# Attention in a two-layer transformer kernel: the context product three heads behind the scores

## The chip, the cores and the metric

The kernel runs on one core of one Trainium2 chip. Its metric is the time on the device in microseconds, from the start of the program to its end. Before the change three runs gave 2274.1, 2275.8 and 2278.2 us; the median is 2275.79 us. The engines are named as the profile names them: PE is TensorE (matrix products; PEld is its loading of weights), DVE is VectorE, ACT is ScalarE, POOL is GpSimd, and SP is SyncE, which only issues transfers (DMAs).

## The reference, cut to what matters

The program is a block of two layers on x of shape 4 x 512 x 512 (4 batch entries, 512 tokens, 512 channels). Layer 0 is a state-space mixer and a mixture of experts; layer 1 is the attention that the change touches and a gated feed-forward net. Ahead of each of these four parts stands a gate computed from a second input by forward and backward scans. The attention, with 16 heads in 4 groups that share keys and values, is:

```python
q = einsum('bsh,he->bse', x, w_q).reshape(b, sq, GROUPS, HPG, KVC)     # 4 groups x 4 heads x 128
kv = einsum('bsh,he->bse', x, w_kv); k, v = split(kv, 2, axis=-1)      # 4 groups x 128 each
scores = einsum('bqgpd,bkgd->bgqpk', q, k) * KVC ** -0.5
scores = where(causal, scores, -inf)
probs = softmax(scores, axis=-1)
ctx = einsum('bgqpk,bkgd->bqgpd', probs, v).reshape(b, sq, HEADS * KVC)
return einsum('bse,eh->bsh', ctx, w_dense)                             # added to x
```

All of it is in 32-bit floats. The output is x after the four parts, each added to it.

## The kernel before, in words

Activations lie with channels on the 128 partitions: x[b] is a tile of 128 x 4 x 512, and h is the gated input of the attention in the same form.

The attention walks a list of 64 heads, `heads_` (line 1737): for each group g of 4, for each batch entry b of 4, for each head i of 4 within the group. One group of one batch entry, four heads, is called a unit here. For each unit `start_group` (line 1585) makes the keys (`pk`, 8 matrix instructions) and values (`pv`, 32). For each head

- `queries` (line 1612) makes the scaled queries, tile `pq`, 8 instructions;
- `scores` (line 1626) works in four steps qi over rows of 128 queries. The causal part only is computed: step qi has (qi + 1) x 128 columns. Each step is a product into a PSUM tile `psc`; VectorE adds the mask and takes the negative row maximum; ScalarE takes the exponential and its row sum; VectorE scales the row and transposes it in blocks of 32 x 32 into an SBUF tile `turned` (two of these). Between the maximum and the exponential stands `nudge()`, which issues one small step of the gates for later parts (their loads kt, ek and ekv on SP, scans on VectorE, exponentials on ScalarE) and sends finished gates off;
- a transpose of 128 x 128 is not complete with blocks of 32. The rest is done on the way through DRAM: four DMAs on POOL's queue write `turned` to a DRAM tile, one of the `turned_d` (line 1661), and one DMA on SP's queue reads it back as `pT` (line 1678). `pT` has two buffers;
- `context` (line 1682) multiplies `pT` with the values, tile `pctx`, 8 instructions, and ScalarE copies the result to `cx`;
- after the fourth head of a unit `dense` (line 1713) multiplies the four `cx` with the dense weights, tile `pd`, 32 instructions, and VectorE adds the result to x[b].

What is delayed against what is written out by hand in the main loop (lines 1756 to 1776). In the pass of head n the queries of head n + 1 come first, then the scores of head n, then `settle()` for the oldest head of the list `held`, once this has more than two: so the context is written two heads behind the scores. `collect()` reads back all that has been written; it stands in `scores` ahead of step 2, so head n - 1 is read back in the middle of the scores of head n. The last two heads of all take another way: their probabilities stay in SBUF and TensorE transposes them.

In group 0 the pass of head 1 of a batch entry also adds the results of the experts to x[b + 1] (`combine`), and the pass of head 2 loads and applies the gate that makes the next h (`gated`, a 1 MB load on SP). The dense weights have one buffer; the next group's are loaded in the pass of head 2 of its first batch entry, after the last `dense` of the group before.

The written order is not the order in which an engine runs. The framework in which the kernel is written orders the instructions of each engine and each queue itself, adds the waits between them, and starts from the order of the code; the trace shows what came out. Where the code says `with after(...)`, the instructions inside are kept behind the last ones of the engines named.

Of the kernel before, what the change touches and what calls it, by code (L numbers as in the profile page):

```python
# [10 lines left out]
F32 = mybir.dt.float32  # L11
# [72 lines left out]
def block_kernel(ctx: ExitStack, tc: tile.TileContext, a: dict, out: bass.AP):  # L84
    nc = tc.nc

    @contextmanager
    def after(*engines):

        with ExitStack() as es:  # L90
            for e in engines:
                last = next(
                    (i for i in reversed(nc.cur_bb.bb.instructions) if i.engine == e.engine), None
                )
                if last is not None:
                    es.enter_context(tc.issue_after(last))
            yield
# [38 lines left out]
    dr = ctx.enter_context(tc.tile_pool(name="spill", bufs=1, space=bass.MemoryType.DRAM))  # L136
# [6 lines left out]
    def ps_mm(name):  # L143
        return ps.tile([P, 512], F32, tag="mm", name=name, bufs=4)

    def ps_tp(name):
        return ps.tile([P, 512], F32, tag="tp", name=name, bufs=2)

    def ps_acc(name):
        return ps.tile([P, 512], F32, tag="acc", name=name, bufs=2)  # L150
# [239 lines left out]
    def nudge():  # L390
        old = list(unsent)
        next(making, None)
        if old:
            send()
# [16 lines left out]
    def gated(l, b, xb, pool, part=slice(0, T), **kw):  # L411
        have((l, b))
        n = part.stop - part.start
        g = pool.tile([P, NC, n], F32, **kw)
        nc.sync.dma_start(out=g, in_=gts[l][b][:, :, part])
        apply_gate(g, xb[:, :, part])
        return g
# [479 lines left out]
    with ExitStack() as ph:  # L897
# [23 lines left out]
        def lend_halves():  # L921

            left = []
            def take():
                if not left:
                    t = sm.tile([P, 8, P], F32, tag="lm", name="lm", bufs=3)
                    left.extend(t[:, i : i + 4, :].rearrange("p a b -> p (a b)") for i in (0, 4))
                return left.pop(0)
            return take
# [15 lines left out]
        turned, lend_turned = [], lend_halves()  # L945
# [556 lines left out]
    def combine(b):  # L1502

        for t in range(NT):
            add_results(b, t, load_results(b, t, nc.sync))
# [46 lines left out]
    with att as ph:  # L1552
# [10 lines left out]
        def load_dense(g):  # L1563
            w = HPG * KVC
            wd = wdp.tile([P, HPG, C], F32, tag="wd", name="wd")
            nc.sync.dma_start(
                out=wd, in_=a["w_dense"][g * w : (g + 1) * w, :].rearrange("(k p) m -> p k m", p=P)
            )
            return wd

        SQ, SLOTS = 32, 13
        QUAD = P // SQ
        turned = [mp.tile([P, QUAD, SLOTS, SQ], F32, name=f"turned{i}") for i in range(2)]
        for blocks in turned:
            for lo, hi in ((1, 3), (5, 6)):
                nc.gpsimd.memset(blocks[:, :, lo:hi, :], 0.0)
        turned_d = [dr.tile([QUAD, SQ, QUAD, SLOTS * SQ], F32, name=f"turned{i}") for i in range(3)]

        hs = [gp.tile([P, NC, T], F32, tag="h", name="h2")] + [None] * (B - 1)
        nc.sync.dma_start(out=hs[0], in_=early_h)  # L1580
# [45 lines left out]
        def scores(u, i, qT):  # L1626

            turn = u.last_row and i >= HPG - 2
            prs = []
            if not turn:  # L1630
                blocks = turned[next(numbers) % 2]
            for qi in range(NT):
                n = (qi + 1) * P
                if qi == 2:
                    collect()
                psc = ps_mm("psc")
                nc.tensor.matmul(  # L1637
                    psc[:, :n], lhsT=qT[:, qi * P : n], rhs=u.kT[:, :n], start=True, stop=True
                )
                nc.vector.tensor_tensor(psc[:, qi * P : n], psc[:, qi * P : n], mask, ALU.add)  # L1640
                nmax = sm.tile([P, 1], F32, tag="nmax", name="nmax", bufs=4)
                nc.vector.tensor_reduce(nmax, psc[:, :n], AX.X, ALU.max, negate=True)  # L1642
                with after(nc.vector, nc.scalar):
                    nudge()
                pr = sm.tile([P, n], F32, tag=f"pr{qi}", name="pr")
                rsum = sm.tile([P, 1], F32, tag="rsum", name="rsum", bufs=4)
                act(pr, psc[:, :n], AF.Exp, bias=nmax, accum_out=rsum)
                nc.vector.reciprocal(rsum, rsum)
                nc.vector.tensor_scalar(pr, pr, rsum, None, ALU.mult)  # L1649
                if turn:  # L1650
                    prs.append(pr)
                    continue
                nc.vector.transpose(  # L1653
                    blocks[:, :, 3 * qi : 4 * qi + 1, :].rearrange("p c k j -> p k c j"), pr
                )
            if turn:
                return prs
            d = turned_d.pop(0)
            turned_d.append(d)
            for r in range(QUAD):  # L1660
                nc.gpsimd.dma_start(  # L1661
                    out=d[:, :, r].rearrange("c i s -> i c s"),
                    in_=blocks[r * SQ : (r + 1) * SQ].rearrange("i c k j -> i c (k j)"),
                )
            away.append(d)
            return d

        away, back = [], {}

        def new_pT():  # L1670
            return sm.tile([P, QUAD, SLOTS, SQ], F32, tag="pT", name="pT")

        def collect():

            while away:
                d = away.pop(0)
                back[id(d)] = pT = new_pT()
                nc.sync.dma_start(
                    out=pT.rearrange("p r k j -> p (r k j)"), in_=d.rearrange("c i r s -> (c i) (r s)")
                )  # L1680

        def context(u, prs):

            if isinstance(prs, list):
                pT = new_pT()
                for qi, pr in enumerate(prs):
                    n = (qi + 1) * P
                    ptp = ps_tp("ptp")
                    for kj in range(qi + 1):
                        nc.tensor.transpose(  # L1690
                            ptp[:, kj * P : (kj + 1) * P], pr[:, kj * P : (kj + 1) * P], ident
                        )
                    nc.any.tensor_copy(
                        pT[:, :, 3 * qi : 4 * qi + 1, :].rearrange("p r k j -> p k r j"),
                        ptp[:, :n].rearrange("p (k r j) -> p k r j", r=QUAD, j=SQ),
                    )
            else:
                collect()
                pT = back.pop(id(prs))
            pctx = ps_acc("pctx")  # L1700
            for kj in range(NT):
                nc.tensor.matmul(  # L1702
                    pctx[:, kj * P :].rearrange("p (q r j) -> p q r j", r=QUAD, j=SQ),
                    lhsT=u.v[:, kj, :],
                    rhs=pT[:, :, 4 * kj : 10 + kj : 3, :].rearrange("p r q j -> p q r j"),
                    start=(kj == 0),
                    stop=(kj == NT - 1),
                )
            cx = sm.tile([P, T], F32, tag="cx", name="cx", bufs=5)
            nc.scalar.copy(cx, pctx)  # L1710
            u.ctxT.append(cx)
# [27 lines left out]
        def begin(n):  # L1739
            g, b, i = heads_[n]  # L1740
            if i == 0:
                if b == 0 and g + 1 < GROUPS:
                    weights[g + 1] = load_group(g + 1)
                groups[g, b] = start_group(g, b, weights[g])
            return groups[g, b], queries(groups[g, b], i)
# [9 lines left out]
        ready, held = begin(0), []  # L1755
        for n, (g, b, i) in enumerate(heads_):
            u, qT = ready
            if g == 0 and i == 1 and b + 1 < B:
                combine(b + 1)
            if g == 2 and i == 0 and b < 3:  # L1760
                to, name = ((ffg_d, "gateT"), (ffu_d, "upT"), (ffd_d, "downT"))[b]
                nc.sync.dma_start(out=to, in_=a[name])
            if g and b == 0 and i == 2:
                dense_w[g] = load_dense(g)
            if n + 1 < len(heads_):
                ready = begin(n + 1)
            if g == 0 and i == 2 and b + 1 < B:
                act.use(act.EXP)
                hs[b + 1] = gated(2, b + 1, x[b + 1], gp, tag="h", name=f"h2_{b + 1}")
                act.use(act.LOG_EXP)  # L1770
            prs = scores(u, i, qT)
            held.append((u, prs))
            if len(held) > 2:
                settle()
        while held:
            settle()
# [213 lines left out]
```

## Time and profile before

| What | us |
|---|---|
| Three runs, median (lowest to highest) | 2275.79 (2274.1 to 2278.2) |
| The profiled execution, its own time | 2278.28 |
| Its span in the profile | 2276.6 |
| Attention stage, from the first pk to the last pd | 1136 to 2031 |
| PE busy in that stage | 860.84 |
| VectorE busy in that stage | 587.84 |
| ScalarE busy in that stage | 340.72 |
| Feed-forward part after it | 2031 to 2277 |
| Median from the issue of a write `turned` to its landing | 3.9 |

The mean granted clock of TensorE over the whole execution is 0.979 of full speed, and 0.99 over the attention stage. The page gives each engine's busy time as a share of the span; a list of waits gives, for each engine and line, what ended its idle time, the total, how many times, and the longest. A timeline gives start, length, engine, line, operation, the tile written and those read, the number of instructions merged into the row, and in brackets the idle time of the engine just before with what ended it. For SP and POOL the rows are the issuing of transfers, not the transfers.

### The profile page before, as it was taken

The page shows a single profiled execution, that of the slowest core. Times are in us where ns is not written, and L with a number is a line of the kernel's source. Part 1 is how long each engine was busy: PE and PEld are TensorE (multiplying, and loading weights), DVE is VectorE, ACT ScalarE, POOL GpSimd, SP SyncE. Part 2 cuts the span into 40 slices and gives each one's busy share as a digit, 9 for nine tenths or more (in the row PEclk, how much of TensorE's full clock was granted, in tenths as well). Part 3 has the DMA queues.
Part 4 walks back from the last instruction along what each step waited for, and adds up shares of the span by engine and source line. Part 5 has one row for each costly group of instructions (what it writes and reads, how often), then busy time and mean ns, then how long its engine had stood idle before and what let it go on. Part 6 is the DMA issues. An engine that isn't in the chain of part 4 may idle for free. (4 is left out here: it accounts for less than half of the span.)

```text
span 2276.6 us, 23890 instructions
## 1 busy us (share of the span) xinstructions
PE 2134.7 (94%) x7528; PEld 1226.5 (54%) x7528; DVE 1524.0 (67%) x3041; ACT 972.2 (43%) x1900; POOL 417.2 (18%) x558
## 2 busy tenths in 40 slices
PE   2879999999999999999989999999999999999998
PEld 1545565555655444444444455555555555568887
DVE  8698989989642665566567766566667765456332
ACT  4476666766732233233254434333333333243222
POOL 4023232421332111111211111111111111100000
PEclk9889989999999999999999999999999999999999
DMA  7542341432523548978675566446545464441100
GB/s 261 169 141 75 102 158 66 153 121 65 186 76 136 190 164 298 341 273 277 209 249 179 172 191 186 139 138 190 167 143 158 139 196 142 131 184 38 37 19 20
DMA packets 112452, 357.38 MB, mean 157 GB/s; under 512 B 14592, under 2 KB 23168, under 8 KB 102912
## 3 DMA queue, kind: packets, MB, share of 16 engines
q1 hardware_dynamic: 87584, 277.26, 36.0%
q0 software_dynamic: 22432, 74.34, 11.1%
q10 hardware_dynamic: 2304, 4.20, 0.5%
q8 instruction: 62, 1.02, 0.2%
q14 instruction: 70, 0.57, 0.1%
HBM read 337.91 MB, written 108.00 MB: 196 GB/s over the span
## 5 line engine op out<-in xcount | busy, mean ns | idle before, releaser
L1661 POOL DMA_DIRECT2D turned<-turned x248 | 135.4, 552 | 713.7 <-DVE turned L1653 435.6
L1615 PE MATMUL pq<-h,wq 128*128 128x512 f32 x512 | 235.4, 597 | 2.0 <-DVE h L404 1.7
L1717 PE MATMUL pd<-cx,wd 128*128 128x512 f32 x512 | 223.3, 594 | 0.0
L128 ACT ACTIVATE pr<-psc,nmax 128x128 f32<-128x128 f32 (+3 forms) x256 | 134.7, 526 | 168.9 <-DVE nmax L1642 168.3
L1048 PE MATMUL pc<-h,wxb 128*128 128x512 f32 x320 | 148.6, 620 | 44.3 <-DVE h L1307 39.2
L1637 PE MATMUL psc<-kT,qT 128*128 128x128 f32 (+3 forms) x512 | 158.2, 442 | 14.5 <-ACT pr L128 14.5
L1702 PE MATMUL pctx<-pT,v 128*128 128x512 f32 (+3 forms) x512 | 153.3, 443 | 13.7 <-DMA pT<-turned 13.3
L1640 DVE TENSOR_TENSOR psc<-psc,mask 128x128 f32<-128x128 f32 x256 | 70.4, 283 | 140.5 <-PE psc L1637 140.3
L1717 PEld LDWEIGHTS pd<-cx,wd 128*128 128x128 f32 x512 | 96.5, 191 | 115.3 <-issue 110.1
L1702 PEld LDWEIGHTS pctx<-pT,v 128*128 128x128 f32 x512 | 98.1, 193 | 98.0 <-issue 67.0
L1615 PEld LDWEIGHTS pq<-h,wq 128*128 128x128 f32 x512 | 94.4, 192 | 100.9 <-issue 93.7
L811 PE MATMUL pg<-w,hT 128*128 128x512 f32 x296 | 136.0, 601 | 6.9 <-ACT hT L784 6.8
L844 PE MATMUL po<-w,yT 128*128 128x512 f32 x296 | 135.9, 600 | 6.2 <-ACT yT L837 6.2
L822 PE MATMUL pn<-w,hT 128*128 128x512 f32 x296 | 133.3, 592 | 0.0
L1725 DVE TENSOR_TENSOR xr<-xr,pd 128x512 f32<-128x512 f32 x64 | 43.8, 685 | 126.6 <-PE pd L1717 126.6
L1637 PEld LDWEIGHTS psc<-kT,qT 128*128 128x128 f32 x512 | 86.2, 192 | 73.6 <-ACT pr L128 31.1
L1048 PEld LDWEIGHTS pc<-h,wxb 128*128 128x128 f32 x320 | 61.8, 198 | 116.4 <-issue 74.5
L1642 DVE TENSOR_REDUCE nmax<-psc 128x1 f32<-128x128 f32 (+3 forms) x256 | 122.7, 480 | 1.9
L1653 DVE STREAM_TRANSPOSE turned<-pr 128x128 f32<-128x128 f32 x248 | 120.8, 498 | 1.4
L1710 ACT COPY cx<-pctx 128x512 f32<-128x512 f32 x64 | 37.2, 581 | 187.5 <-PE pctx L1702 187.5
L1119 PE MATMUL pz<-wzt,h 128*128 128x512 f32 x256 | 115.2, 598 | 0.3 <-ACT st L1220 0.3
L1267 PE MATMUL po<-wot,yT 128*128 128x512 f32 x256 | 115.2, 604 | 0.0
(343 smaller groups left out, 4198.0 us busy)
## 6 DMA issues: line engine op xcount, KB each, us to landing
w<-in_w1x SPq DMA_DIRECT2D x76, 1024.0 KB
turned<-turned POOLq DMA_DIRECT2D x248, 208.0 KB, 3.9
pT<-turned SPq DMA_DIRECT2D x62, 832.0 KB
w<-in_w2x SPq DMA_DIRECT2D x38, 1024.0 KB
wb<-in_b1x SPq DMA_DIRECT2D x38, 512.0 KB
lm<-cs SPq DMA_DIRECT2D x32, 512.0 KB
kt<-in_fT SPq DMA_DIRECT2D x62, 256.0 KB
ek<-ek SPq DMA_DIRECT2D x62, 256.0 KB
```

Source lines behind the costliest of these rows:

```text
L128: nc.scalar.activation(*args, **kw)
L811: nc.tensor.matmul(pg, lhsT=hT[:, k, :], rhs=self.w1[s][0][:, k, :], start=(k == 0), stop=(k == NC - 1))
L822: nc.tensor.matmul(pn, lhsT=hT[:, k, :], rhs=self.w1[s][1][:, k, :], start=(k == 0), stop=(k == NC - 1))
L844: nc.tensor.matmul(po, lhsT=yT[:, j, :], rhs=self.w2[s][:, j, :], start=(j == 0), stop=(j == NI - 1))
L1048: nc.tensor.matmul(pc, lhsT=wxb[:, k, m * P : (m + 1) * P], rhs=h[:, k, :], start=(k == 0), stop=(k == NC - 1),)
L1615: nc.tensor.matmul(pq, lhsT=u.wq[:, k, i * KVC : (i + 1) * KVC], rhs=u.h[:, k, :], start=(k == 0), stop=(k == NC - 1),)
L1637: nc.tensor.matmul(psc[:, :n], lhsT=qT[:, qi * P : n], rhs=u.kT[:, :n], start=True, stop=True)
L1642: nc.vector.tensor_reduce(nmax, psc[:, :n], AX.X, ALU.max, negate=True)
L1653: nc.vector.transpose(blocks[:, :, 3 * qi : 4 * qi + 1, :].rearrange("p c k j -> p k c j"), pr)
L1661: nc.gpsimd.dma_start(out=d[:, :, r].rearrange("c i s -> i c s"), in_=blocks[r * SQ : (r + 1) * SQ].rearrange("i c k j -> i c (k j)"),)
L1702: nc.tensor.matmul(pctx[:, kj * P :].rearrange("p (q r j) -> p q r j", r=QUAD, j=SQ), lhsT=u.v[:, kj, :], rhs=pT[:, :, 4 * kj : 10 + kj : ...
L1717: nc.tensor.matmul(po, lhsT=dense_w[u.g][:, i, m * P : (m + 1) * P], rhs=u.ctxT[i], start=(i == 0), stop=(i == HPG - 1),)
```

## The change

`held` now keeps three heads, so the context of head n - 3 is written after the scores of head n. `collect` takes a number of written heads that it leaves for later; in `scores` it stands ahead of step 0 and leaves one, so head n - 2 is read back at the start of the scores of head n. `context` calls `collect` only when its own probabilities have not been read back yet. A fourth DRAM tile holds the written probabilities. The dense weights of a group are loaded in the pass of head 3 instead of head 2, after the last `dense` of the group before, which comes one head later too.

```diff
-        turned_d = [dr.tile([QUAD, SQ, QUAD, SLOTS * SQ], F32, name=f"turned{i}") for i in range(3)]
+        turned_d = [dr.tile([QUAD, SQ, QUAD, SLOTS * SQ], F32, name=f"turned{i}") for i in range(4)]
...
             for qi in range(NT):
                 n = (qi + 1) * P
-                if qi == 2:
-                    collect()
+                if qi == 0:
+                    collect(1)
...
-        def collect():
+        def collect(rest=0):
 
-            while away:
+            while len(away) > rest:
                 d = away.pop(0)
                 back[id(d)] = pT = new_pT()
...
             else:
-                collect()
+                if id(prs) not in back:
+                    collect()
                 pT = back.pop(id(prs))
...
-            if g and b == 0 and i == 2:
+            if g and b == 0 and i == 3:
                 dense_w[g] = load_dense(g)
...
             prs = scores(u, i, qT)
             held.append((u, prs))
-            if len(held) > 2:
+            if len(held) > 3:
                 settle()
```

## The prediction

> **What bounds the kernel now.** I read the page first, for the engine that is busy, then TensorE's waits inside the attention stage, then TensorE's instructions in order of time, and last the queues that feed the one wait that matters.
>
> ```profile
> span 2276.6 us, 23890 instructions
> PE 2134.7 (94%) x7528; PEld 1226.5 (54%) x7528; DVE 1524.0 (67%) x3041; ACT 972.2 (43%) x1900; POOL 417.2 (18%) x558
> ```
>
> TensorE (PE) is busy for 94% of the span, so a reordering that leaves its work alone can win at most its idle time and what it loses in clock. The table of stretches gives the attention stage (1136 to 2031 us) 860.84 us of PE in 895: 34.2 us idle. The waits of that stage, PE alone, name two causes:
>
> ```profile
> PE psc L1637 <- ACT pr L128: 14.5, 18, 3.2
> PE pctx L1702 <- DMA pT<-turned: 13.3, 8, 3.5
> ```
>
> Scores wait for a PSUM bank that the softmax still reads (14.5 us), and the context product waits for the probabilities read back from DRAM (13.3 us in 8 waits). The change aims at the second. One of its eight, in PE's order of time:
>
> ```profile
> 1396.27 13.90 PE L1717 MATMUL pd<-cx,wd 128*128 128x512 f32 x32
> 1410.01 2.32 PE L1702 MATMUL pctx<-pT,v 128*128 128x512 f32 x8
> 1412.16 3.60 PE L1593 MATMUL pk<-h,wkv 128*128 128x512 f32 x8
> 1415.60 3.73 PE L1601 MATMUL pv<-wkv,h 128*128 128x128 f32 x32
> 1419.17 1.88 PE L1615 MATMUL pq<-h,wq 128*128 128x512 f32 x4
> 1420.89 2.32 PE L1637 MATMUL psc<-kT,qT 128*128 128x128 f32 x8
> 1423.05 2.32 PE L1702 MATMUL pctx<-pT,v 128*128 128x512 f32 x8
> ...
> 1449.67 3.87 PE L1702 MATMUL pctx<-pT,v 128*128 128x512 f32 x8 [3.54 <-DMA pT<-turned]
> 1453.38 13.90 PE L1717 MATMUL pd<-cx,wd 128*128 128x512 f32 x32
> ```
>
> Call a unit k one group of four heads of one batch entry, (k,i) its head i. From dense to dense PE runs four contexts, four scores, four queries, one pk and pv. Between 1420.89, the scores of (k,3), and the wait at 1449.67, the context of (k,3), it ran the scores of three further heads. The written order has only two there, so the instruction order already departs from the code: PE ran (k+1,2) ahead of a context that was late. Why it is late stands in the queues of POOL (writes) and SP (loads):
>
> ```profile
> 1430.19 2.17 POOL L1661 DMA_DIRECT2D turned<-turned  x4 [22.15 <-DVE psc L1640]
> ```
>
> ```profile
> 1432.83 0.32 SPq L247 DMA_DIRECT2D ek<-ek  x1
> 1440.96 0.33 SPq L240 DMA_DIRECT2D kt<-in_fT  x1
> 1441.51 0.79 SPq L1678 DMA_DIRECT2D pT<-turned  x1
> 1450.10 0.32 SPq L249 DMA_DIRECT2D ekv<-ekv  x1
> ```
>
> The write ended issuing at 1432.4 and lands a median 3.9 us later, at 1436.3. The read left only at 1441.51: ahead of it in SP's queue stood a gate load, kt, and SP's own waits put that one down to VectorE (`eu`, line 278). Then the read took 8 us. From the start of the scores to their context: 28.8 us. The late, gate-free periods show PE without a gap, 51.8 us from dense to dense.
>
> **The change, part by part.**
>
> *Context one head later.* No instruction is added or removed. The context of (k,3) and the dense product now follow the scores of (k+1,2) in the code, which is where PE already runs them. What really moves is the context of (k,0): it stood right after dense (1410.01) and now stands behind pk, pv, one pq and the scores of (k,3). So those scores start one context sooner after dense, 2.16 us (the chain of waits gives 2.16 for these 8 matmuls), while the context of (k,3) keeps its place. Its probabilities get 2.16 us more. The eight waits and what is left:
> first unit, 0.90 and 1.98: no dense has run yet, so nothing of this shift applies, 0 taken (at best 2.88).
> 1326, 0.35; 1394, 1.56; 1510, 1.32; 1565, 1.30: all under 2.16, gone, 4.53 together (at 1565 0.86 of pk had been run ahead, which leaves the 1.30).
> 1450, 3.54: 2.16 gone.
> 1618, 2.37: here PE had already run all of pk and two of pv ahead (3.66 us), so an earlier context only shrinks that filling, 0.
> Sum 6.7 us; ends 0 (order unchanged) and 13.3.
>
> *Clock.* The 3.54 wait is followed by a context of 3.87 us instead of 2.32, and the stretch 1446 to 1454 has a granted clock of 0.79. After waits of 1.3 to 1.6 it takes 2.40 at clock 1.00. So 1.5 us more goes with that wait. The stretch 1615 to 1623 (0.81, after 2.37) stays, since that wait stays. Ends 0 and 5 (three such places).
> [...]
>
> *Scores waiting for the softmax.* Between the scores of (k,3) and of (k+1,0) PE now has one context more to do, so VectorE and ScalarE get 2.16 us to free banks. Per period the gain is capped at 2.16 or PE's idle time in it. From the stretches between denses, 1285 to 1834 without the 1618 one, idle is 0.35, 1.80, 3.54, 2.58, 2.13, 1.20, 1.68, 0.59, 0.29; capped 12.3, of which 6.7 is counted above. The rest, 5.6, is the upper end, 0 the lower; I take half, 2.8, because VectorE is 65 to 75% busy there and some of these waits are its own pace (gate work sits between the score steps).
>
> *Reads one half head later in the code.* 62 reads, unchanged in number, now written two steps later, past the gate loads of two `nudge` calls and, in six units, past the 1 MB loads of h or dense weights on SP. SP waited 252.5 us in 55 reads for the write: it reaches them early, so a later place in the code costs nothing as long as SP still issues them when the write lands. Cover: the read is used a head later as well. If it slips behind the next gate load it costs what the first rival says. Both buffers of pT stay: a read must wait for the context two heads earlier. For (k,2) that context moves from right after dense to 12.6 us later, leaving 2 x (3.44 + 2.16) + 2.16 = 13.4 us until use, against reads of 5.3 to 10.1 us: hidden with 3 us or more to spare, 0.
>
> *Dense weights one head later.* Three 1 MB loads (line 1566). The buffer was freed at 1410.01, the load left at 1410.20, and the next dense came 43 us later; both ends move by one head. SP stands on this wait 28.9 us in three loads, as before, with pT reads behind it; these now have a head more. 0.
>
> *A fourth DRAM buffer, and `collect` only if needed.* POOL waited 435.6 us for VectorE's transposes and for no buffer: 0. Head 61 of 64 is now fetched from the final drain: its read left at 1990.4 and was used at 2004.5. Behind the 16 feed-forward loads (to 1999.9) it would land 3.4 us late; it still stands ahead of them in the code, so 0, upper end 3.4.
>
> Sum 6.7 + 1.5 + 2.8 = 11.0 us. The profiled execution took 2278.28 us (1.7 around its span) and lies 2.5 above the median of the three runs; against its own time the sum gives 2267.3, against the median 2275.8 it gives 2264.8.
>
> **The rivals.**
>
> *The read slips behind the next gate load (slower).* SP issues in order, and the reads are held up by gate loads today. One place further back, the read of 1441.51 leaves after the ekv of 1450.10, 9.1 us later. The same step at the other five late reads, to the next SP load, is 6.5 (1320), 4.8 (1386), 3.5 (1502), 6.4 (1555), 5.3 (1611): 35.6 in all. Less six times 2.16 that is 22.6: 2298. It decides from two such slips on, which eat the gain. For it: the read is written behind two more gate steps. Against: kt precedes the read though its data came later, so SP's order follows an expected readiness rather than the code.
>
> *The order comes out the same (no change).* PE already runs the scores of (k+1,2) first; if it also keeps the context of (k,0) right after dense, nothing moves: 2276. Against: pk stands ahead of it in the code now.
> [...]
>
> *Softmax takes over (slower, small).* PE freed of pT waits meets the banks sooner; the waits of 14.5 us rise by what the others lose, so that nothing is left of the 11, and the gaps of the first unit (11.9 us idle before 1224) grow by half, 6 us, as the first context comes a head later: 2282.
>
> *All goes.* Every pT wait, the psc waits of the periods and 5 us of clock: 13.3 + 5.6 + 5 = 23.9, 2252.
>
> **How the numbers follow.** Forecast 0.42, all goes 0.10 (both faster); same order 0.16; slip 0.20; softmax 0.12. A difference under 0.2%, 4.6 us, is about what a measurement of this kernel can't tell from none. So faster 0.52, same 0.16, slower 0.32. The time is the forecast's, 2265; its own range is 2257 to 2271. The 80% range reaches 2254 below (leaving out part of all goes) and 2285 above (softmax in, and the slip where it strikes a few times).
>
> **What would show it.** Right: after each dense, pk, pv, pq and scores come before a context; pctx waits for DMA fall from 13.3 to some 6 us or less; periods before 1690 shorten by about 2 us. Wrong: pT reads on SP directly behind an ekv or ek rather than a kt, pctx waits beyond 4 us, psc waits above 20 us, or a context still right behind dense.

## The result, and the profile after

The changed kernel took 2269.09 us against 2278.29 us before, each the median of 22 runs; the ratio is 0.9961, with a 95% interval of 0.9948 to 0.9973. Two later comparisons of the same two kernels gave 0.9983 (0.9967 to 0.9999) and 0.9955 (0.9938 to 0.9973). So the change is worth some 4 to 10 us of 2278, and the forecast of 11 us had the right sign and a size a little above that. The way there was another one.

The profiled execution of the changed kernel took 2262.92 us, one of its fastest; that of the kernel before, 2278.28 us, stands at its median. The first lines of its page:

```profile
span 2260.9 us, 23897 instructions
PE 2123.0 (94%) x7528; PEld 1219.8 (54%) x7528; DVE 1524.8 (67%) x3040; ACT 971.5 (43%) x1901; POOL 418.4 (19%) x558
```

The second and third profiles of the kernel before, used further down, come from executions that were slow as a whole (2288.7 and 2290.7 us, where 19 others on that chip took 2271.7 to 2284.8), so they are given beside the first and nothing rests on them alone.

The span is 15.7 us shorter than before, but that is not all the change's. The first pk of the attention starts at 1131.3 instead of 1136.3 us, and everything ahead of it is the same code. What belongs to the change is the attention stage, first pk to last pd: 894.7 us before, 883.9 after, 10.8 less.

PE's busy time fell as well, by 11.7 us over the program, though it ran the same 7528 products. That is the first sign that the clock had a part. PE's waits in the attention stage after the change:

```profile
PE psc L1637 <- ACT pr L128: 12.0, 12, 3.2
PE pctx L1703 <- DMA pT<-turned: 9.6, 4, 3.3
```

The waits for the probabilities fell from 13.3 us in eight places to 9.6 in four. The forecast had 13.3 - 6.7 = 6.6. Here is the unit whose wait was shown before, in PE's order of time:

```profile
1385.02 13.90 PE L1718 MATMUL pd<-cx,wd 128*128 128x512 f32 x32
1398.75 3.60 PE L1593 MATMUL pk<-h,wkv 128*128 128x512 f32 x8
1402.19 3.73 PE L1601 MATMUL pv<-wkv,h 128*128 128x128 f32 x32
1405.76 3.60 PE L1615 MATMUL pq<-h,wq 128*128 128x512 f32 x8
1409.19 2.32 PE L1637 MATMUL psc<-kT,qT 128*128 128x128 f32 x8
1411.35 2.32 PE L1703 MATMUL pctx<-pT,v 128*128 128x512 f32 x8
...
1432.44 2.32 PE L1637 MATMUL psc<-kT,qT 128*128 128x128 f32 x8
1438.07 2.39 PE L1703 MATMUL pctx<-pT,v 128*128 128x512 f32 x8 [3.31 <-DMA pT<-turned]
```

The order is the one that was forecast: pk, pv, pq and scores stand ahead of the first context. Yet the late context still waits 3.31 us, 3.54 before. It is followed by matmuls at full speed (2.39 us for the eight, at a clock of 1.00 from 1434 to 1442; 3.87 before, at 0.79 from 1446 to 1454). These are the queues of POOL and SP in the same unit:

```profile
1418.49 2.17 POOL L1661 DMA_DIRECT2D turned<-turned  x4 [23.52 <-DVE psc L1640]
```

```profile
1429.26 0.33 SPq L240 DMA_DIRECT2D kt<-in_fT  x1
1429.81 0.82 SPq L1678 DMA_DIRECT2D pT<-turned  x1
1438.36 0.32 SPq L249 DMA_DIRECT2D ekv<-ekv  x1
```

The read leaves right behind the same kt as before, 20.6 us after the first scores of its head (1409.19), as it did before (1441.51 - 1420.89). It did not slip behind the ekv.

**How idle time and clock divide.** The table of stretches gives, for any stretch, PE's busy time and the granted clock. I cut the attention stage into 120 stretches of about 7.45 us and added up two things: the time in which PE was idle, and (1 - clock) times the length, called clock lost below. Stage length less these two comes to 845 to 848 us in all fourteen executions in the table below, whichever kernel it is, so the two account for the differences to within 3 us. In this first pair PE idle goes from 33.8 to 30.3, and clock lost from 13.1 to 6.0: of the 10.8 us, 3.5 is idle time and 7.1 is clock.

### The profile page after: what moved, and what is told of

The parts are those of the page before. It is cut to its first block, busy times and chain, and to the rows that moved or that the text cites. A ratio compares the mean times of both kernels' runs of the same rounds, so it can differ in the third digit from the quotient of the medians.

```text
span 2260.9 us, 23897 instructions
## 1 busy us (share of the span) xinstructions
PE 2123.0 (94%) x7528; PEld 1219.8 (54%) x7528; DVE 1524.8 (67%) x3040; ACT 971.5 (43%) x1901; POOL 418.4 (19%) x558
## 4 chain that ended last, share of the span: by engine, by line
PE 36%; DVE 9%; DMA 2%; ACT 2%; issue 1%; SPq 0%; DVEq 0%; ACTq 0%
PE pd L1718 9%; PE pq L1615 5%; PE pctx L1703 3%; PE psc L1637 3%; PE pk L1593 3%; PE pv L1601 3%; PE pfo L1821 2%; PE pfo L1820 2%; PE pfg L1820 2%; PE pfg L1821 2%; PE pfu L1821 2%; PE pfu L1820 2%; DVE turned L1653 2%; DVE nmax L1642 2%; DMA pT<-turned 1%; DVE pr L1649 1%
## 5 line engine op out<-in xcount | busy, mean ns | idle before, releaser
L811 PEld LDWEIGHTS pg<-w,hT 128*128 128x128 f32 x296 | 56.2, 194 | 75.9 <-issue 66.3
```

Source lines behind the costliest of these rows:

```text
L811: nc.tensor.matmul(pg, lhsT=hT[:, k, :], rhs=self.w1[s][0][:, k, :], start=(k == 0), stop=(k == NC - 1))
```

## The experiments

All kernels below, with the attention stage of one profiled execution of each. "pT waits" is PE's idle time before contexts, with the number of places. "In units 0 to 2" is the part of the clock lost between 45 and 230 us after the start of the stage. Medians are compared only with the kernel before on the same chip, by the ratio.

| Kernel | stage us | PE idle | clock lost | in units 0 to 2 | pT waits | ratio to before |
|---|---|---|---|---|---|---|
| before | 894.7 | 33.8 | 13.1 | 3.4 | 13.3 (8) | 1 |
| before, second | 900.3 | 37.0 | 16.8 | 6.9 | 16.5 (9) | one execution |
| before, third | 899.9 | 35.0 | 19.7 | 10.1 | 15.4 (9) | one execution |
| after | 883.9 | 30.3 | 6.0 | 0 | 9.6 (4) | 0.9961 |
| after, second | 888.5 | 30.6 | 9.7 | 0 | 9.1 (4) | 0.9983 |
| after, third | 883.6 | 29.6 | 6.1 | 0 | 8.6 (4) | 0.9955 |
| late reads only | 893.8 | 32.8 | 14.7 | 5.1 | 14.0 (8) | 1.0000 |
| context later, early reads | 884.6 | 30.6 | 6.1 | 0 | 9.2 (4) | 0.9966 |
| context later in group 0 only | 889.9 | 31.9 | 9.8 | 0 | 8.7 (5) | 0.9974 |
| context later in groups 1 to 3 only | 894.8 | 32.9 | 14.6 | 3.4 | 13.6 (8) | 0.9994 |
| before, POOL reads | 893.3 | 32.1 | 14.8 | 8.6 | 9.5 (8) | 0.9998 |
| after, POOL reads | 881.9 | 23.6 | 11.2 | 5.1 | none | 0.9958 |
| after, POOL reads, second | 881.6 | 23.7 | 11.0 | 5.1 | none | 0.9944 |
| after, mixed reads | 876.8 | 22.6 | 6.4 | 0 | none | 0.9917 |

Theory A is the forecast: the scores start sooner after dense, and so the waits for pT shrink. Theory B, formed on the first pair of profiles: the waits stay behind SP's gate loads, and what changed is mostly the clock.

### The same kernels again

No edit; the changed kernel twice more and the kernel before twice more.

> The changed kernel once more, nothing altered, for a second execution in profile. In the first pair of profiles the attention stage is 10.8 us shorter: PE idle 33.9 to 30.3 us (3.5), and the clock that was not granted, (1 - clock) times time, 13.1 to 6.0 us (7.1). Theory A, the forecast (earlier scores shorten the waits for pT): pT waits of 9.6 us were an accident, here 6 us or less. Theory B (the late read stays behind a gate load of SP and the waits stay; the rest was clock): pT waits 9 to 10 us in 4 places again, the clock lost in the attention stage anywhere between 6 and 13 us, the time 2262 to 2276 and moving with it.

> The changed kernel a third time, nothing altered. Theory B: PE idle 30 to 31 us in the attention stage, pT waits 9 to 10 us, clock lost there 5 to 13 us; the ratio to before between 0.995 and 0.999, as the two comparisons so far gave 0.9961 and 0.9983. Theory A: pT waits of 6 us or less.

> The kernel before once more, nothing altered, for a second profile. Theory B: PE idle in the attention stage is a property of the instruction order and comes out at 33 to 35 us again with 13 to 14 us of pT waits in 8 places; the clock lost there is an accident of which gaps are followed by a slow clock and may lie anywhere between 5 and 15 us. If the clock loss belongs to this kernel too, it is 12 to 15 us again.

> The kernel before a third time, for a third profile, as for the second: PE idle 33 to 35 us, pT waits 13 to 14 us; the clock lost in the attention stage 5 to 15 us if it is an accident, 12 to 15 us if it belongs to this order.

Theory A fell: the pT waits of the changed kernel are 9.1 and 8.6 us in four places, not 6 or less. Of theory B one half stands and one had to be mended. Idle time is a property of the order: 29.6 to 30.6 in three executions after, 33.8 to 37.0 before (the expectation of 33 to 35 was too narrow). But the clock is no accident: before loses 13.1 to 19.7 us (the two later profiles more than either expectation had), after 6.0 to 9.7, and the ranges don't meet. With only the first profile before and that of the kernel with late reads only, which has its context in the old place, it is 13.1 and 14.7 against the same 6.0 to 9.7. I lean on where the clock is lost rather than on how much: in units 0 to 2 all these executions with the context in the old place lose some and none after does.

### The two halves of the change

Context three heads behind, but the reads where they were:

```diff
-                if qi == 0:
-                    collect(1)
+                if qi == 2:
+                    collect()
```

> The context three heads behind, the fourth DRAM buffer and the dense weights as in the change, but the reads stay ahead of step 2 of the next head's scores, as before. If the place of the reads in the code matters (rival: the later read is what changed something), it lies nearer the kernel before, 2275 to 2280, or is slower. Theory B, with SP's order set by readiness and not by the code: within 3 us of the changed kernel, 2266 to 2272, and the reads leave SP behind the same gate loads.

It measured 2266.45 us, 0.9966 (0.9953 to 0.9979), with the idle time, waits and clock of the changed kernel, and its late read leaves SP behind the same kt, again 20.6 us after the scores. The other half, the kernel before with only the reads moved:

```diff
-                if qi == 2:
-                    collect()
+                if qi == 0:
+                    collect(1)
...
-            while away:
+            while len(away) > rest:
...
-                collect()
+                if id(prs) not in back:
+                    collect()
```

> Only the reads moved: they stand ahead of step 0 and leave one head, the context stays two heads behind, three DRAM buffers. Theory B: no gain, 2276 to 2281, pT waits 13 us or more, since the context keeps its place. The rival that the later reads free SP's queue: the gain of the change or part of it, 2268 to 2273.

It measured 2275.73 us, 1.0000 (0.9986 to 1.0013), with the idle time and the clock of the kernel before. So the whole gain comes with the context's place (and with what moves along with it, the fourth DRAM tile and the later load of the dense weights, which were not run alone); the later reads do nothing that can be measured, neither good nor bad.

### Where in the attention the gain is

The number of heads held is made to depend on the group, the rest is the changed kernel:

```diff
-            if len(held) > 3:
+            while len(held) > (3 if g == 0 else 2):
                 settle()
```

> The changed kernel, but with the context three heads behind only in group 0 (first quarter of the attention, with the experts' results and the next gates in it), two behind after it. So far the attention stage takes 894.7 to 899.4 us before (three profiles, PE idle 33.8 to 37.0, clock lost 13.1 to 19.7) and 883.6 to 888.5 after (three, idle 29.6 to 30.6, clock lost 6.0 to 9.7). Theory C (most of the gain is clock, at two places in group 0 near 70 and 135 us after the stage's start, where several short gaps follow each other, and at one near 315 us, where one gap is over 3.5 us): the two places of group 0 are at full clock, the third is slow again; clock lost 8 to 11 us, idle 32 to 34, stage 888 to 891, time about 2270. Theory A (gain from the pT waits of groups 0 to 2): stage 893 or more.

It measured 2271.03 us, 0.9974 (0.9960 to 0.9988): clock lost and stage as theory C said, idle 31.9. (The stage of the kernel before, to the end of its last pd, is 894.7 to 900.3 us; the upper end above is 0.9 short.) The other part has `3 if g > 0 else 2`.

> The other part: two heads behind in group 0, three behind in groups 1 to 3. Theory C: the two places of group 0 are slow again, 3.5 us together at least, the gap near 315 us is under 3.5 us and costs no clock: clock lost 9 to 14 us, idle 31 to 33, stage 890 to 893, time about 2272. Theory A: nearly the whole gain of the change, stage 886 to 888.

It measured 2274.28 us, 0.9994 (0.9976 to 1.0013): a stage of 894.8 us, 2 us longer than expected, and 14.6 us of clock lost where 9 to 14 was expected. Its gap near 315 us lost 3.4 us of clock although it was 3.39 us long, and in group 0 it lost 1.7 us near 85 us after the stage's start, not near 70, and 1.7 us near 140. So what can be measured is in the first quarter of the attention, where the experts' results and the next gates are worked in; for the other three quarters no gain is shown. The pT waits agree: 8.7 us in five places with the context later in group 0 only, 13.6 in eight with it later in groups 1 to 3 only. Stretches of 15 us show the clock. First the one with the context later in group 0 only, 64 to 79 us after the stage's start and near its gap of 3.60 us in group 1; the columns are length, then busy time and instructions of PE, PEld, DVE, ACT and POOL, then clock, DMA share and GB/s:

```profile
1203.00:1218.00 15.00, 13.01 (x50) 7.35 (x49) 13.16 (x34) 5.02 (x12) 4.08 (x8) 1.00 0.85 282
1446.00:1461.00 15.00, 11.40 (x24) 5.67 (x24) 7.23 (x18) 4.33 (x10) 2.26 (x5) 0.77 0.70 229
```

The one with the context later in groups 1 to 3 only, in unit 1 and at its gap of 3.39 us:

```profile
1270.00:1285.00 15.00, 11.04 (x31) 5.09 (x30) 14.79 (x38) 5.48 (x14) 2.94 (x6) 0.89 0.81 235
1447.00:1462.00 15.00, 11.61 (x24) 5.74 (x24) 7.58 (x22) 5.34 (x13) 4.35 (x8) 0.77 0.91 274
```

Full clock stands where the order of units 0 and 1 is the new one. What that order does differently is seen in unit 1. First the kernel before, then the changed one, 15 us each:

```profile
1266.00:1281.00 15.00, 11.05 (x31) 5.23 (x30) 14.90 (x38) 5.21 (x14) 3.35 (x7) 0.89 0.81 241
1258.00:1273.00 15.00, 11.89 (x36) 5.93 (x37) 14.03 (x36) 6.87 (x17) 2.77 (x5) 1.00 0.81 223
```

PE's rows there in the kernel before:

```profile
1268.33 0.91 PE L1637 MATMUL psc<-kT,qT 128*128 128x384 f32 x2 [0.23 <-ACT pr L128]
1270.81 1.12 PE L1637 MATMUL psc<-kT,qT 128*128 128x512 f32 x2 [1.57 <-ACT pr L128]
1273.46 0.63 PE L1496 MATMUL pcb<-ident,rr 128*128 128x128 f32 x4 [1.53 <-DVE rr L1491]
1274.72 0.68 PE L1496 MATMUL pcb<-ident,rr 128*128 128x128 f32 x4 [0.62 <-DVE rr L1491]
```

and in the same unit after the change:

```profile
1258.53 0.91 PE L1637 MATMUL psc<-kT,qT 128*128 128x384 f32 x2 [1.00 <-ACT pr L128]
1259.28 2.32 PE L1703 MATMUL pctx<-pT,v 128*128 128x512 f32 x8
1262.74 1.13 PE L1637 MATMUL psc<-kT,qT 128*128 128x512 f32 x2 [1.15 <-ACT pr L128]
1264.68 0.63 PE L1496 MATMUL pcb<-ident,rr 128*128 128x128 f32 x4 [0.81 <-DVE rr L1491]
1265.93 0.63 PE L1496 MATMUL pcb<-ident,rr 128*128 128x128 f32 x4 [0.63 <-DVE rr L1491]
```

Before, three gaps of 1.57, 1.53 and 0.62 us follow each other with some 0.6 to 1.1 us of work between them: softmax and the experts' results are both late and there is nothing to put in. After, a whole context, 2.32 us, stands between the waits, and the two long gaps are 1.15 and 0.81. The context was moved out of the place behind dense, where PE had plenty to do, to one where it had not. That the order in these units decides the clock is shown by the two kernels of this section and by the last one below; that it does so through gaps that stand closer together is argued from these rows. PE's share alone does not tell it: in 7.45 us from 1270.45 before PE is busy for 4.94 us at a clock of 0.82, in 7.45 us from 1257.94 after for 4.82 us at 1.00.

### The reads on another queue

The reads of pT are issued from POOL's queue in place of SP's, first in the changed kernel and then in the kernel before:

```diff
-                nc.sync.dma_start(
+                nc.gpsimd.dma_start(
                     out=pT.rearrange("p r k j -> p (r k j)"), in_=d.rearrange("c i r s -> (c i) (r s)")
```

> The changed kernel with the reads of pT issued from POOL's queue, right behind the writes, instead of SP's, where they stand behind gate loads that wait for VectorE. Theory B: the reads leave when the write has landed, some 5 us sooner, the pT waits fall from 9.6 to under 2 us and the time to 2258 to 2264. If the transfer itself or VectorE's pace is the limit, the pT waits stay at 8 us or more and the time within 3 us of the changed kernel.

> The changed kernel with the reads of pT on POOL's queue, once more, since its first comparison (0.9958) can't be told from those of the changed kernel (0.9955 to 0.9983). Idle 23 to 24 us again in the attention stage and no pT wait over 1 us; clock lost there 9 to 13 us, which eats over half of the idle time won; the ratio 0.994 to 0.997. If the clock loss of its first profile was an accident, 6 to 8 us lost and 0.993 or below.

> The kernel before with the reads of pT issued from POOL's queue, the context two heads behind. Theory B (the wait is SP's queue): the pT waits fall from 13.3 us to under 3, and most of the gain of the changed kernel with POOL reads (2263.5) is had without moving the context: 2263 to 2268. If the context's place is needed as well, the pT waits stay above 6 us and the time at 2270 or more.

With the change the waits are gone and idle time is 23.6 and 23.7 us, at 2263.53 us (0.9958, interval 0.9941 to 0.9975) and 2264.34 us (0.9944, 0.9925 to 0.9964). Without it there was no gain, 0.9998, and 9.5 us of pT waits. So the time came out as expected for the one and not for the other, and the reason that I gave is not what the rows show. In the unit followed so far the read left hardly sooner. POOL's and then PE's rows of the changed kernel with POOL reads:

```profile
1424.86 2.22 POOL L1661 DMA_DIRECT2D turned<-turned  x4 [3.97 <-DVE psc L1640]
1433.49 2.18 POOL L1661 DMA_DIRECT2D turned<-turned  x4 [6.41 <-DVE psc L1640]
1435.66 0.56 POOL L1678 DMA_DIRECT2D pT<-turned  x1
```

```profile
1415.56 2.32 PE L1637 MATMUL psc<-kT,qT 128*128 128x128 f32 x8
...
1438.81 2.32 PE L1637 MATMUL psc<-kT,qT 128*128 128x128 f32 x8
1441.94 3.70 PE L1593 MATMUL pk<-h,wkv 128*128 128x512 f32 x8 [0.81 <-ACT pr L128]
1445.48 3.73 PE L1601 MATMUL pv<-wkv,h 128*128 128x128 f32 x32
```

The read leaves 20.1 us after its scores, against 20.6 from SP: there it stood behind a gate load, here behind the writes of the next head. What is new is PE's order. The keys and values of the next unit, 7 us, now stand ahead of the late context (1449.91) instead of behind dense, and cover the wait. How the framework came to that order from a change of queue was not tried. Nor does this run show that SP's gate loads alone made the waits.

The clock shows here too: both executions lose 5.1 us in units 0 to 2, where the changed kernel loses none, and so most of the 6 to 7 us of idle time won over the changed kernel is lost again. Hence the last kernel, reads on SP in the first two batch entries of group 0 and on POOL from there on:

```diff
+        reader = [nc.sync]
...
-                nc.sync.dma_start(
+                reader[0].dma_start(
...
+            if g or b > 1:
+                reader[0] = nc.gpsimd
             prs = scores(u, i, qT)
```

> The changed kernel with the reads of pT on SP for the first two batch entries of group 0 and on POOL's queue from there on. Both kernels with POOL reads throughout have PE idle 23.6 and 23.7 us, no pT wait, stages of 881.9 and 881.6 us, but lose 11.2 and 11.0 us of clock, 5 of it near 67 and 135 us after the stage's start, where the changed kernel loses none. If the order in those two units is what decides the clock: clock lost 6 to 7 us, idle 23 to 26, stage 877 to 880, time 2258 to 2262, ratio to before 0.992 to 0.995. If the clock loss comes with the POOL reads as such, it stays at 10 to 11 us and the stage at 881 or more.

It measured 2257.10 us against 2277.85, a ratio of 0.9917 (0.9897 to 0.9937): no clock lost in units 0 to 2, idle 22.6, stage 876.8. Time, stage and idle time are each a little better than the ranges expected. Against the kernel before the gain is clear; the changed kernel it was not run beside, but its interval lies just below all three of the changed kernel's, whose lowest end is 0.9938.

## Why the prediction was right or wrong

*Bound and order: right.* PE's idle time and clock are what can be won, and the first context moved behind the scores of (k,3). The forecast said that PE already ran the scores of (k+1,2) before the context of (k,3); it did, and does.

*"Those scores start one context sooner after dense, 2.16 us": the step that failed.* The 2.16 took for granted that pk, pv and a full pq stand between dense and scores, before and after. Before it was not so: PE had put off a part of pq or all of it until behind the scores, or had run some of pk ahead. In the units of 1394, 1450, 1510, 1565 and 1618 the scores of the fourth head came 11.4, 10.7, 10.7, 9.0 and 8.1 us after the end of dense, and come 10.3, 10.3, 10.3, 7.7 and 10.3 after. So the head start is 1.1, 0.4, 0.4, 1.3 and -2.2 us, nowhere 2.16.

Nor do the waits follow the head start alone, because what PE does between those scores and the late context changed too: a context came in and queries went out. In the four units with waits left (1394, 1450, 1510 and 1618) the late context started 27.2, 28.8, 31.9 and 28.9 us after the scores, and starts 27.3, 28.9, 31.7 and 28.1 after them now. Without the wait this was 25.6, 25.2, 30.6 and 26.5 us and is 25.6, 25.6, 29.7 and 25.6. So 1.56, 3.54, 1.32 and 2.37 became 1.74, 3.31, 2.00 and 2.55. The 1.30 at 1565 did go, but not by the head start: PE comes to that context 4.4 us sooner after the scores than before, and the read leaves 16.9 us after them where it left after 20.1.

From the five units the forecast took 6.3 us and got 0.5. From the three waits ahead of them it took 0.35 (for 0.90 and 1.98 in the first unit it took 0) and got all 3.2. The sum, 13.3 to 9.6, is a gain of 3.7 where 6.7 was forecast, and that it came even so near is luck.

*Clock: the term that was mis-sized.* 1.5 us forecast, 7.1 in the first pair. The 3.87 us context was gone as foreseen, though its wait had hardly shrunk. Three more places of 1.7 us went that the sum had not counted. One is that behind the 2.37 us wait, which was taken to stay; the wait did stay (2.55), and in the second execution after, behind 2.33 us, the place was slow again. The other two are in units 0 and 1, behind waits for softmax and for the experts' results and one pT wait of 0.90; these are the ones that no execution after has.

*Softmax waits: 14.5 to 12.0, 2.5 us, where 2.8 was taken.* The size is right, though the 2.8 was half of a range whose reason was not tested. It is not the net gain that the sum made of it: idle time as a whole fell by only 3.5 in the first pair, since pk waits for banks (0.5 to 1.5) and pd for the copies of contexts (0 to 1.6) took some back.

*Later reads, dense weights, the fourth buffer: 0.* For the reads this is right; alone they measured 1.0000. The other two were not run alone, and nothing in the rows speaks against 0 (SP's wait ahead of the three loads of dense weights is 25.2 us after, 28.9 before). SP's waits for the write fell from 252.5 us to 146.9 and its waits for the context two heads earlier rose from 28.8 to 104.6; no wait of PE for pT grew out of it, as all four that are left are those of fourth heads.

*The rivals.* The slip behind the next gate load did not happen in the unit shown: the read stands behind the same kt, and it does so too when the reads keep their old place in the code, so the order of SP's queue did not follow that place. At 1565 the read does stand behind an ekv now, which the forecast took for a sign of being wrong, but it leaves sooner than before (16.9 us after the scores, 20.1 before). The same order is refuted by PE's rows. Nor did the late read wait for a buffer of pT: its buffer is free from 1421.4 and the read leaves at 1429.81. Softmax taking over is refuted: those waits fell. That the total fits the forecast is luck: too much idle time and too little clock cancelled.

## What to carry to other kernels

Ahead of a change of order, measure from the real instruction order where each engine has nothing to do, not from the order of the code: a product moved from a full place to an empty one paid here (a clock of 0.89 before and 1.00 after in the 15 us of unit 1), one that was moved past work that the order had already put off did not (0.5 us of pT waits in the five units, where 6.3 were forecast). Short waits that followed each other closely went with a lower clock here, beside the idle time (1.57, 1.53 and 0.62 us in 15 us at a clock of 0.89; with the change 1.15, 0.81 and 0.63 us at 1.00), so add up (1 - granted clock) over the stage beside the idle time, and take several executions before either is read as a cause. When a wait vanishes after a queue is changed, look whether the transfer left sooner or whether something else now covers it.

## What the runs showed of the hardware that was not expected

The clock is lost in near-equal portions: in the tables of stretches the slow places behind the attention stage's first 45 us cost 1.71 or 3.43 us each, but for one of 5.14, in the kernel before with POOL reads, and four slow stretches in a row in the third profile of the kernel before, 6.85 together. In the first profile before there are four of 1.71; in its second, two of 1.71 and two of 3.43; in the changed kernel's second profile, two of 1.71. Why they come in this size no run shows.

The length of a gap alone does not tell whether it costs clock. In the unit near 315 us every gap of 3.5 us or more before a context lost clock (3.54, 3.64, 3.52, 3.62 and 3.60). Of those of 3.3 to 3.45 in the same unit, 3.31, 3.35, 3.40 and 3.43 lost none and 3.39 did. Clusters of shorter ones lose it too: in unit 1, gaps of 1.57 and then 1.08 to 1.53 us close behind it did so in all three executions before and with late reads only (there 1.57 and 1.18). Why one gap of 2.2 to 3.0 us loses the clock (2.24, 2.33, 2.37, 2.59 and 2.62) and another does not (2.50, 2.55 and 2.98) stays open.
